# Second expert layer of a two-layer graph block: what the late row fetches wait for, when the rank products run, and where the last sums are loaded

## The chip, the cores and the metric

The kernel runs on one core of a Trainium2 chip. The metric is the device time of one execution in microseconds (us), as the median of several runs. The profile is one further execution, with the hardware profiler on. The engines are called as the profile calls them: PE (matrix products; PEld is its weight load), DVE (vector), ACT (scalar), POOL (GpSimd) and SP (the engine that does nothing here but issue transfers). A small q behind an engine's name (SPq) means its instruction sequencer, which waits, branches and issues DMAs.

## What is computed

A block of two layers over 2708 rows of 256 numbers. Each layer normalizes the rows, mixes them by an attention over a 0/1 adjacency matrix, adds the result to the rows, normalizes again, and adds the output of a mixture of eight experts, in which each row takes its two best experts. The change is in the experts of the second layer:

```python
def _L1_ffn_ref(x, gate_w, gate_b, W1, b1, W2, b2):
    logits = xf @ gate_w + gate_b
    probs = jax.nn.softmax(logits, axis=-1)
    top2_vals, top2_idx = jax.lax.top_k(probs, 2)
    cw = jnp.zeros((N, Ee), dtype=xf.dtype).at[jnp.arange(N)[:, None], top2_idx].add(top2_vals)
    def step(acc, params):
        w1, bb1, w2, bb2, we = params
        h = jax.nn.gelu(xf @ w1 + bb1, approximate=False)
        y = h @ w2 + bb2
        return (acc + we[:, None] * y, None)
...
x = x + _L1_gnn_ref(_layernorm(x, axis=-1), adj, ...)
x = x + _L1_ffn_ref((_layernorm(x, axis=-1))[None], ...)[0]
```

Here the hidden width is 512, and all numbers are float32.

## The kernel before

**Routing.** The rows form 22 tiles of 128 (the last has 20 rows). `route` (line 1437 on) is a Python generator, one per tile. It normalizes the tile, finds the two best experts of each row, and counts with two small matrix products (L1533 and L1534, the *rank products*) how many rows of earlier tiles and of this tile go to each expert. From the counts it works out a place for each row, adds the tile to the running count `seen` (L1542), and sends the rows with two indirect DMAs from POOL (L1551) to `disp`, a table in DRAM with one region per expert. Each `yield` ends a step. A `Line` holds the generators: its `step()` runs one step of each that is under way, oldest first, and starts a new one at most every `gap` steps. In the second layer most tiles are routed during the attention; the last five reach their rank products beside the experts' slots, while the flag `slots_run` is set, where `line.step()` is called twice per slot and `gap` is 2. There the power of e (L1526) is taken on POOL, and DVE sums it up in L1531.

**Slots.** The experts' work is cut into slots, each of 128 rows of one expert. The second layer has 47 that always run, numbered 0 to 46 here (`often` is 47), and up to 23 more behind a branch that these data don't take. `slot(s, s1)` issues in this order: the first product (`up`, sixteen matmuls of L1835, then four GELUs of L1843 on ACT), the transposed rows of the next slot (`turned`, L1808 on DVE), a step of the line, `down` of the slot before (eight matmuls of L1851, the scaling L1857 on DVE into one of three buffers `y`, and an indirect DMA from POOL, L1863, that writes the 128 result rows to `xd1` in DRAM), a second step of the line, and whatever is listed for this slot in `self.then`. Inside `down`, before the scaling, `fetch` issues what later slots need: rows for up to six slots ahead (`fetch_rows`: SP reads where the chunk begins, L1753, and issues four DMAs of L1760 into `xg` and one of L1766 into `who`) and the weights for three slots ahead (`fetch_weights`, L1741 on POOL, which moves nothing where the buffer already holds that expert).

**Order.** PE, ACT, DVE and SP run in the order in which the Python code issues; each engine works through its own list in order, and an instruction that waits holds up all behind it on that engine. POOL's order is the scheduler's.

**Late slots.** Slots 0 to 19 take rows of the first 14 tiles, slots 20 on take the rest. So the rows of slot 20 may be fetched only when all rows are routed. When the line is empty, `place_grid` works out on DVE which rows the slots from 20 on take, two steps per slot, and makes eight indirect DMAs on POOL (`pad_rows`, L1570) that fill up the last chunk of every expert. `self.written` collects the DMAs that must have landed: the routed rows, the pads, and also the results of L1863. In `fetch_rows`, slots 0 and 20 wait for all that `self.written` holds at that time (`behind_written`). For slot 20 these include the results of slots 0 to 12.

**Sums.** Each row's two results lie in two halves of `xd1`. For the first 16 tiles (four groups of four, `whole_`) eight loads of 512 KB are issued from SP in slot 40's `then` (L2048, `load`); they wait for the results of slots 0 to 38. In `then` of slots 43 to 46 DVE adds each group to the kept rows (`add`, L2061 and L2062) and SP stores it (`store`, L2065). The other six tiles (`rest`) form four groups. They are loaded after `experts1.run`, and so behind the branch, from SP and ACT, into the buffers of the first four groups.

**The branch.** After slot 46 every engine loads the number of used slots into a register (L1960) and jumps over the 23 conditional slots (`tc.If`, L1976). At the place it jumps to, the engines raise the semaphores by what the skipped instructions would have raised, so that the code behind sees the same counts on both ways. SP does that for the eight semaphores that its and ACT's DMAs use, and each raise waits for what was issued on that semaphore before; POOL does it for its own DMAs with one instruction of L1976 (INC_SWDGE_SEM).

Of the kernel before, what the change touches and what calls it, by code (L numbers as in the profile page):

```python
# [106 lines left out]
def adj_ffn_kernel(ctx: ExitStack, tc: tile.TileContext, a: dict, out: bass.AP):  # L107
    nc = tc.nc
# [1020 lines left out]
    class Experts:  # L1129
        def __init__(self, layer, hidden, packed_weights, gate_bias, own_norm, xd, disp, early):  # L1130
# [4 lines left out]
            nc.vector.memset(self.seen, 0.0)  # L1135
            self.routed, self.begun, self.pads = 0, False, []
            self.slots_run = False
            self.written = []
            self.groups = [f"written{layer}", f"late{layer}", f"apart{layer}", f"after{layer}", f"rows{layer}", f"summed{layer}"]
            self.early = early  # L1140
            self.side = "right" if own_norm else "left"
# [21 lines left out]
            s0 = n + size * RING  # L1163
# [258 lines left out]
                tc.declare_no_dep(start.ins, group=self.groups[2], reason="other rows of xd")  # L1422
                tc.add_to_no_dep_group(self.groups[3], start.ins)

        def behind_written(self, start, last=True, but=0):
            for ins in self.written[: len(self.written) - but]:
                tc.add_manual_dep(
                    start.ins, ins.name,
                    mybir.DependencyInfo(
                        mybir.DependencyClass.Sync, mybir.DependencyReason.DATA  # L1430
                    ),
                    reason="rows written",
                )
            if last:
                self.written = []

        def route(self, t, x, logits=None):

# [90 lines left out]
            yield  # L1529
            if self.slots_run:  # L1530
                nc.vector.tensor_reduce(den[:r, 0:1], p[:r, :k], AX.X, ALU.add)  # L1531
            ps = misc.tile([P, GROUP, P], F32, name="misc").rearrange("p g n -> p (g n)")
            nc.tensor.matmul(ps[:, :E], before, sel, start=True, stop=False)  # L1533
            nc.tensor.matmul(ps[:, :E], ones, seen, start=False, stop=True)  # L1534
# [263 lines left out]
        def slots(self, two, ps_mm, ps_acc, line):  # L1798
# [49 lines left out]
            def down(s, w, who, hT, bias2, then):  # L1848
# [12 lines left out]
                if not own_norm:  # L1861

                    start = nc.gpsimd.indirect_dma_start(  # L1863
                        xd[:], at, y, None, bounds_check=2 * N - 1, oob_is_err=False
                    )
                    for i in (2, 5):
                        tc.declare_no_dep(
                            start.ins, group=self.groups[i], reason="other rows of xd"
                        )
                    tc.add_to_no_dep_group(self.groups[2], start.ins)  # L1870
                    self.written.append(start.ins)
                    return
                start = nc.gpsimd.indirect_dma_start(  # L1873
                    xd[:], at, y, None, bounds_check=N - 1, oob_is_err=False, compute_op=ALU.add
# [98 lines left out]
            if own_norm:  # L1973
                others(often)
                return
            with tc.If(used > often):  # L1976
# [26 lines left out]
    with tc.tile_pool(name="mask", bufs=1) as mp, ExitStack() as first_masks:  # L2003
# [16 lines left out]
        with tc.tile_pool(name="sum", bufs=1, side="right") as pool:  # L2020
# [24 lines left out]
            def load(parts_, queues, early=0):  # L2045
                for i, (t, n, r) in enumerate(parts_):
                    for j, queue in enumerate(queues):
# [4 lines left out]
                            )  # L2052
                            tc.add_to_no_dep_group(experts1.groups[5], start.ins)
                        if i == 0:
                            experts1.behind_written(
                                start, last=(j == 1 and parts_ is rest), but=int(early)
                            )

            def add(t, n, r):
                y, y1 = results(t, n, r)  # L2060
# [3 lines left out]
            def store(t, n, r):  # L2064
                nc.sync.dma_start(rows_of(out, 0, t, n, r), results(t, n, r)[0])  # L2065

            def again():
                load(whole_, (nc.sync, nc.sync))
                for x in whole_:
                    add(*x)  # L2070
                    store(*x)

            experts1.again = again
            s0 = experts1.sum_behind + 2
            experts1.then = {s0: [partial(load, whole_, (nc.sync, nc.sync), 1)]}
            for i, x in enumerate(whole_):
                experts1.then[s0 + 3 + i] = [partial(add, *x), partial(store, *x)]
            experts1.run(line)
            load(rest, (nc.sync, nc.scalar))
            for x in rest:  # L2080
                add(*x)
                store(*x)
# [37 lines left out]
```

## Time and profile before

| what | value |
|---|---|
| median of three runs | 1191.05 us (1186.0 to 1194.85) |
| profiled execution, its own time | 1177.48 us |
| its span, first to last instruction | 1175.8 us |
| PE busy over the span | 1125.0 us (96%) |
| first matmul of slot 0 of the second layer's experts | at 976.9 us of the span |
| first matmul of slot 46 | at 1150.94 us |
| scaling of slot 46's results on DVE (L1857) | at 1157.45 us |
| first of the last loads on SP (L2048) | at 1165.33 us |
| last addition on DVE (L2062) | at 1172.69 us |

The table gives the span's own clock: 0 is the first instruction. The profiled execution was shorter than the median of the other three by 13.6 us, about 1%; the work and its order are the same in all of them. Between slots 28 and 43 a slot takes 3.51 us, and PE has no pause; this is the pace of the part where nothing is late.

### The profile page before, as it was taken

To read this page: it belongs to the slowest core of one execution; us is meant where nothing else is said; L and a number is where in the kernel's file an instruction comes from. 1 tells how busy PE (TensorE), PEld (TensorE's weight loads), DVE (VectorE), ACT (ScalarE), POOL (GpSimd) and SP (SyncE) were. 2 spreads that over 40 slices of the span, in tenths; PEclk is the share of its full clock that TensorE was granted. 3 is DMA by queue.
4 is the path that set the end of the run, shared out by engine and by line. 5 is a ranking of instruction groups with operands and counts; after the bars stand their busy time and mean duration, and the time that the engine had idled before them with its cause. 6 is when DMAs were issued, how large, how long until landed. Compare 5 with 4: busy or idle time off the path is not lost. (4 is left out here: it accounts for less than half of the span.)

```text
span 1175.8 us, 20858 instructions
## 1 busy us (share of the span) xinstructions
PE 1125.0 (96%) x6421; PEld 912.2 (78%) x6421; DVE 647.7 (55%) x2405; ACT 415.4 (35%) x1232; POOL 430.3 (37%) x519
## 2 busy tenths in 40 slices
PE   8989999999999999999999999998999998998993
PEld 5665666666666666789999999997899997898992
DVE  5565777786876867643222222222876777622224
ACT  3222222222222222433333333332777673344441
POOL 3001212121212122453434343423754557865552
PEclk9999999999999999999999999999999999999997
DMA  9678676867745658579675936543000517577346
GB/s 224 130 163 211 169 183 167 237 168 181 215 128 149 155 140 317 154 206 262 181 197 151 339 83 187 122 159 86 28 1 33 211 56 238 123 241 231 79 131 229
DMA packets 198661, 195.88 MB, mean 167 GB/s; under 512 B 90939, under 2 KB 181524, under 8 KB 192520
## 3 DMA queue, kind: packets, MB, share of 16 engines
q1 hardware_dynamic: 173242, 118.18, 39.7%
q0 software_dynamic: 24256, 70.81, 19.0%
q10 hardware_dynamic: 1038, 5.40, 1.3%
q8 instruction: 55, 0.90, 0.3%
q14 instruction: 70, 0.57, 0.2%
HBM read 246.19 MB, written 66.15 MB: 266 GB/s over the span
## 5 line engine op out<-in xcount | busy, mean ns | idle before, releaser
L1835 PEld LDWEIGHTS mm<-xe,ring 128*128 128x128 f32 x2192 | 260.6, 194 | 15.8 <-DVE xe L1808 5.8
L1835 PE MATMUL mm<-xe,ring 128*128 128x128 f32 x2192 | 263.9, 278 | 5.5 <-DVE xe L1808 3.9
L1843 ACT ACTIVATE hT<-mm,ring 128x128 f32<-128x128 f32 x548 | 156.6, 369 | 287.6 <-issue 157.2
L1851 PE MATMUL acc<-ring,hT 128*128 128x256 f32 x1096 | 252.1, 380 | 0.0
L1851 PEld LDWEIGHTS acc<-ring,hT 128*128 128x128 f32 x1096 | 201.6, 191 | 24.2 <-issue 0.4
L650 PEld LDWEIGHTS acc<-v,p 128*128 128x128 f32 (+1 forms) x880 | 160.0, 190 | 62.4 <-issue 37.0
L650 PE MATMUL acc<-v,p 128*128 128x257 f32 (+1 forms) x880 | 202.7, 383 | 0.0
L586 PE MATMUL s<-g,xnT 128*128 128x512 f32 x420 | 200.3, 597 | 0.6 <-DVE mT L605 0.6
L1551 POOL DMA_INDIRECT disp<-row,to x88 | 92.0, 1045 | 256.9 <-DVE x L670 125.5
L1857 DVE SCALAR_TENSOR_TENSOR y<-acc,who,bias 128x256 f32<-128x256 f32 x92 | 44.3, 481 | 254.6 <-PE acc L1851 232.9
L288 POOL TENSOR_TENSOR ln_rs<-ln_rs,minus_half 128x2 f32<-128x2 f32 x88 | 68.7, 782 | 172.9 <-DVE ln_rs L284 120.4
L598 ACT ACTIVATE p<-s 128x512 f32<-128x512 f32 x105 | 62.7, 597 | 194.8 <-PE s L586 178.7
L930 PE MATMUL acc<-parts,m 128*128 128x266 f32 x924 | 126.2, 293 | 0.0
L930 PEld LDWEIGHTS acc<-parts,m 128*128 128x128 f32 x924 | 117.1, 185 | 4.1 <-ACT raw L957 0.9
L586 PEld LDWEIGHTS s<-g,xnT 128*128 128x128 f32 x420 | 76.8, 190 | 55.1 <-issue 50.3
L1741 POOL DMA_INDIRECT ring<-L_ffn_packed,weight_row x76 | 80.2, 1055 | 92.4 <-PE acc L1851 61.8
L601 DVE SCALAR_TENSOR_TENSOR p<-p,mT 128x512 f32<-128x512 f32 x100 | 71.0, 710 | 75.3 <-ACT p L598 75.2
L1873 POOL DMA_INDIRECT xd<-y,who x45 | 71.2, 1583 | 111.3 <-DVE xe L1814 50.2
L897 ACT CAST m<-mT 128x512 fp32r<-128x512 fp8e4 (+4 forms) x168 | 71.8, 475 | 9.7 <-PE acc L930 6.3
L1863 POOL DMA_INDIRECT xd<-y,who x47 | 50.3, 1071 | 48.6 <-DVE y L1857 44.8
L272 DVE SCALAR_TENSOR_TENSOR row<-x,wr_rows 128x256 f32<-128x256 f32 x128 | 54.4, 425 | 3.3
L1814 DVE TENSOR_SCALAR xe<-xe_raw,ring 128x128 f32<-128x128 f32 x90 | 27.7, 352 | 40.2 <-DMA ring<-L_ffn_packed,weight_row 39.2
(337 smaller groups left out, 1073.1 us busy)
## 6 DMA issues: line engine op xcount, KB each, us to landing
adj<-in_adj_dram SPq DMA_DIRECT2D x100, 256.0 KB
L_ffn_packed<-in_L_ffn_W_dram SPq DMA_DIRECT2D x32, 512.0 KB
xg<-disp SPq DMA_DIRECT2D x368, 32.0 KB
L_ffn_packed<-in_L_ffn_W_dram SPq DMA_DIRECT2D x32, 256.0 KB
neighbours<-mT SPq DMA_DIRECT2D x5, 1408.0 KB
mT<-neighbours SPq DMA_DIRECT2D x5, 1408.0 KB
ring<-L_ffn_packed SPq DMA_DIRECT2D x3, 2182.0 KB
xin<-in_x_dram SPq DMA_DIRECT2D x42, 128.0 KB
```

The source lines that it names most:

```text
L288: nc.gpsimd.tensor_tensor(rs[:r, 1], rs[:r, 0], minus_half[:r], ALU.pow)
L586: nc.tensor.matmul(ps[:kr, :nb], xnT[:, c, k0 : k0 + kr], g[:, c, :nb], start=(c == 0), stop=(c == DC - 1 and k < KEYS),)
L601: nc.vector.scalar_tensor_tensor(p, p, LARGEST, mask, op0=ALU.min, op1=ALU.mult)
L650: nc.tensor.matmul(accs[j][:r], p[keys, q0 : q0 + r], v[keys, k, :], start=(k == 0), stop=(k == NT - 1),)
L897: nc.scalar.copy(m[:, : q1 - q0], MASKS[b].of_key(mTs[b], k)[:, q0 - b * BN : q1 - b * BN],)
L930: nc.tensor.matmul(acc[:r], masks[t], parts[:, k, i], start=(k == 0 and i == 0), stop=False,)
L1551: nc.gpsimd.indirect_dma_start(disp[:], bass.IndirectOffsetOnAxis(ap=to[:r, j : j + 1], axis=0), rows2[:r, j], None,)
L1741: nc.gpsimd.indirect_dma_start(w, None, packed[:], bass.IndirectOffsetOnAxis(ap=self.weight_row[:, s : s + 1], axis=0), bounds_check=E * P ...
L1835: nc.tensor.matmul(ps[:, i, :], w[:, c * hidden + f * P : c * hidden + (f + 1) * P], xe[:, c, :], start=(c == 0), stop=(c == DC - 1),)
L1843: nc.scalar.activation(hT[:, f, :], ps[:, i, :], AF.Gelu, bias=w[:, b1 + f : b1 + f + 1])
L1851: nc.tensor.matmul(ps, hT[:, f, :], w[:, w2 + f * D : w2 + (f + 1) * D], start=(f == 0), stop=(f == hc - 1),)
L1873: start = nc.gpsimd.indirect_dma_start(xd[:], at, y, None, bounds_check=N - 1, oob_is_err=False, compute_op=ALU.add)
```

## The change

Five things are done to the second layer's experts:

- `self.results` is a list of its own for the DMAs that write results. `self.written` keeps the routed rows and pads. So slot 20's row fetch waits for rows and pads alone, and the loads of the sums wait for results alone.
- In `route`, for the tiles of the second layer that are routed beside the slots, one more `yield` stands ahead of the rank products. They, and all that follows in the tile (the places, `seen`, the two DMAs of L1551), come one step of the line later.
- The loads of the last four groups (`load(rest, ...)`) are issued ahead of `tc.If`, behind the loading of the register, as `self.ending()`.
- In the branch's body, which these data skip, the last four groups are loaded again, from SP.
- The additions and stores of the first four groups are listed for slots 42 to 45 in place of 43 to 46. Their loads stay with slot 40.

```diff
-            self.written = []
+            self.written, self.results = [], []
...
-        def behind_written(self, start, last=True, but=0):
-            for ins in self.written[: len(self.written) - but]:
+        def behind_results(self, start, but=0):
+            self.behind(start, self.results[: len(self.results) - but])
+
+        def behind_written(self, start, last=True):
+            self.behind(start, self.written)
+            if last:
+                self.written = []
+
+        def behind(self, start, written):
+            for ins in written:
                 tc.add_manual_dep(
...
             if self.slots_run:
                 nc.vector.tensor_reduce(den[:r, 0:1], p[:r, :k], AX.X, ALU.add)
+            if self.slots_run and not own_norm:
+                yield
             ps = misc.tile([P, GROUP, P], F32, name="misc").rearrange("p g n -> p (g n)")
             nc.tensor.matmul(ps[:, :E], before, sel, start=True, stop=False)
             nc.tensor.matmul(ps[:, :E], ones, seen, start=False, stop=True)
...
-                    self.written.append(start.ins)
+                    self.results.append(start.ins)
...
+            self.ending()
             with tc.If(used > often):
...
                         if i == 0:
-                            experts1.behind_written(
-                                start, last=(j == 1 and parts_ is rest), but=int(early)
-                            )
+                            experts1.behind_results(start, but=int(early))
...
                 for x in whole_:
                     add(*x)
                     store(*x)
+                load(rest, (nc.sync, nc.sync))
 
             experts1.again = again
+            experts1.ending = partial(load, rest, (nc.sync, nc.scalar))
             s0 = experts1.sum_behind + 2
             experts1.then = {s0: [partial(load, whole_, (nc.sync, nc.sync), 1)]}
             for i, x in enumerate(whole_):
-                experts1.then[s0 + 3 + i] = [partial(add, *x), partial(store, *x)]
+                experts1.then[s0 + 2 + i] = [partial(add, *x), partial(store, *x)]
             experts1.run(line)
-            load(rest, (nc.sync, nc.scalar))
             for x in rest:
                 add(*x)
                 store(*x)
```

`self.sum_behind` is 38, so `s0` is 40.

More of the change, by code (lines that the diff above doesn't have):

```diff
@@ L1433, in behind_written @@
                 )
-            if last:
-                self.written = []
         def route(self, t, x, logits=None):
```

## The prediction

> **What bounds the kernel now.** I read the page first, then the busy time by windows of the second layer's experts, then the chain of waits there, then the waits of single engines, last the timeline of the end. The page names PE:
>
> ```profile
> PE 1125.0 (96%) x6421; PEld 912.2 (78%) x6421; DVE 647.7 (55%) x2405; ACT 415.4 (35%) x1232; POOL 430.3 (37%) x519
> ```
>
> So nothing is to be won but where PE pauses. The change touches only what lies behind 976.9 us; the windows there (PE, PEld, DVE, ACT, POOL busy, PE clock, DMA share, GB/s) show where PE is not full:
>
> ```profile
> 1036.00:1052.00 16.00, 16.00 (x110) 14.99 (x109) 3.34 (x8) 7.44 (x25) 11.23 (x11) 1.00 0.99 359
> 1052.00:1064.00 12.00, 12.00 (x86) 11.36 (x85) 3.52 (x8) 4.87 (x16) 6.43 (x7) 1.00 0.43 94
> 1064.00:1080.00 16.00, 14.20 (x96) 12.64 (x94) 3.03 (x7) 6.49 (x20) 8.25 (x9) 1.00 1.02 341
> 1140.00:1157.00 17.00, 16.35 (x107) 14.67 (x105) 12.37 (x16) 6.16 (x21) 7.71 (x5) 1.00 0.96 354
> 1157.00:1162.00 5.00, 0.00 (x0) 0.00 (x0) 0.93 (x2) 0.00 (x0) 1.12 (x2) 0.64 0.43 140
> 1162.00:1165.00 3.00, 0.00 (x0) 0.00 (x0) 0.00 (x0) 0.00 (x0) 0.00 (x0) 0.50 0.03 8
> ```
>
> Two bursts of weights fill the DMA engines (1036 to 1052 and 1064 to 1080); PE pauses in the second only. Behind 1157 there are 8 us with almost no work at all. The chain says what the pause in the second burst hangs on; SP's and DVE's waits give the size:
>
> ```profile
> 1038.96 7.67 DMA xd<-y,who
> 1046.82 6.82 DMA xg<-disp
> ...
> 1062.22 6.05 DMA xg<-disp
> ...
> 1069.63 7.78 DMA xg<-disp
> 1077.43 5.96 DMA xg<-disp
> ```
> ```profile
> SPq L1760 <- DMA xd<-y,who: 5.8, 1, 5.8
> ```
> ```profile
> DVE xe L1808 <- DMA xg<-disp: 15.2, 7, 4.5
> ```
>
> Slot 12's result landed 7.67 us after its issue, SP stood 5.8 us for it, and every later row fetch was late by that. The timeline has the price: slots 24 to 28 begin at 1069.75, 1073.65, 1079.00, 1084.01 and 1087.6, where 3.51 us is the pace, so 0.39 + 1.84 + 1.50 + 0.1 = 3.8 us are lost.
>
> The end, by the timeline of DVE and of the two loading queues, and by the instructions of L1976:
>
> ```profile
> 1140.53 0.48 DVE L1857 SCALAR_TENSOR_TENSOR y<-acc,who,bias 128x256 f32<-128x256 f32 x1 [2.68 <-PE acc L1851]
> 1140.93 0.43 DVE L1808 STREAM_TRANSPOSE xe<-xg 128x256 f32<-128x256 f32 x1
> 1144.04 0.48 DVE L1857 SCALAR_TENSOR_TENSOR y<-acc,who,bias 128x256 f32<-128x256 f32 x1 [2.68 <-PE acc L1851]
> 1144.44 1.22 DVE L2061 TENSOR_TENSOR y<-y,kept 128x1024 f32<-128x1024 f32 x1
> 1157.45 0.48 DVE L1857 SCALAR_TENSOR_TENSOR y<-acc,who,bias 128x256 f32<-128x256 f32 x1
> ```
> ```profile
> 1165.33 1.73 SPq L2048 DMA_DIRECT2D y<-xd  x4
> 1165.40 1.98 ACTq L2048 DMA_DIRECT2D mT<-xd  x4
> 1168.77 0.69 DVE L2061 TENSOR_TENSOR y<-y,kept 128x512 f32<-128x512 f32 x1 [10.84 <-DMA mT<-xd]
> ```
> ```profile
> L1976 SPq EVENT_SEMAPHORE  x9: 17/17/17, 1162.1 to 1162.6; - x9
> L1976 PEldq COMPARE_BRANCH  x1: 4557/4557/4557, 1156.3 to 1156.3; - x1
> L1976 SPq COMPARE_BRANCH  x1: 50/50/50, 1158.3 to 1158.3; - x1
> L1976 POOLq INC_SWDGE_SEM  x1: 1617/1617/1617, 1163.4 to 1163.4; - x1
> ```
>
> Slot 46's result lands at 1161.96 by the trace's completion events, but the loads start only when POOL's INC_SWDGE_SEM is done (1163.4 + 1.6 = 1165.0). SP is back from its branch 3.75 us after it (1158.3 to 1162.1).
>
> **The change part by part.** I write times on the clock of before and carry a shift.
>
> *Row fetch of slot 20.* Its wait was the whole 5.8 us: SP was ready at 1040.5, routed rows and pads had landed by 1028.6. SP then runs 5.8 us ahead. In a burst a fetch takes SP some 4.6 us instead of 2.97 (L1753 starts of fetches 25 to 29: 1064.22 to 1082.61), because each of the eight DMA semaphores must be free again; so 5.8 us are 1.3 fetches, and in the quiet part 1.3 x 3.18 us (mean pace of fetches 29 to 46) = 4.1 us. Of the 3.8 us lost I give back 3.5: rows of slot 28, issued near 1072 and landing some 8 us later, become the latest, about 0.3 us late. Ends: 3.8, all of it, and 1.3, if the rows of slot 28 land when those of 27 do now (1083.4, 2.5 us too late). The weights are not next: those of slot 29, the last of the burst, land at 1082.9, needed at 1087. PE: -3.5.
>
> [...]
>
> *Rank products.* For five tiles two matmuls (0.17 us each), seven short DVE operations (some 1.2 us) and two POOL DMAs (1.03 us each) come half a slot later; nothing is added. PE's waits for them between 976 and 1010 are:
>
> ```profile
> PE misc L1533 <- DVE sel L1523: 3.2, 3, 1.6
> PE misc L1534 <- DVE seen L1542: 1.5, 2, 0.7
> ```
>
> Most is covered: PE would have waited for the transposed rows anyway (1.6 us at 987.9: rows ready 988.27, products done 988.1). Visible are 0.5 us each at 994.3 and 1004.5. But DVE still waits for POOL's power in L1531 (7.3 us in 4 waits), and POOL works without a gap there. The last tile ends behind the check of slot 6, so placing starts in slot 7, one slot (3.5 us) later: rows of slots 20 on are placed at 1026.5, SP reads them at 1040.5; the weight rows at 1028.5, POOL reads them at 1028.3, cover gone, 0.2 us off the path. I take -0.3. Ends: -1.0 (both visible waits), and +2 if POOL puts results behind the pads; a result that waits like this already cost DVE 3.95 us and PE 0.8 us at slot 13.
>
> *Early sums a slot sooner.* Same eight additions (1.22 us each), four stores. The first would start behind slot 41's scaling, at 1140.93 - 3.5 - 0.3 = 1137.1. Its rows: loads start behind SP's last fetch, 1139.71 - 4.1 = 1135.6; the first landed 3.8 us after its issue (1139.71 to 1143.50, by the completion events), so 1139.4. DVE waits 2.3 us, and the transposed rows of slot 44 are queued behind it. These now start at 1140.93 with 2.4 us to spare before slot 44's matmuls at 1143.84, and the additions use 2.45 up. So the wait is PE's: +2.3. The second load of the group lands 1.3 us after the first, in time; later groups come every 2.6 us against 3.5 us per slot. Ends: 0, if SP gets all 5.8 us, to +6.4, if it keeps none of its lead. On the other side the last addition no longer stands before slot 46's scaling: PE ends at 1156.35, the scaling began at 1157.45, -1.0. Sum at that scaling: -3.5 - 0.3 + 2.3 - 1.0 = -2.5, so 1154.95. The stores leave SP a slot sooner and are landed when the loads reuse their buffers.
>
> *Last loads ahead of the branch.* They wait for slot 46's result only: 0.75 us to its issue, then 2.4 us (as 1134.27 to 1136.68; it took 3.75 beside the last store): 1158.1. Four DMAs each on SP and ACT, 0.3 us to the first and 1.75 on SP; behind them SP has its branch, then the raising of the semaphores, then the stores; ACT nothing that matters. The additions are written after a second load inside the skipped branch, so I read them as waiting for SP's raising: 1158.1 + 2.1 + 3.75 + 0.6 = 1164.6. The last load lands 6.7 us after the release (1165.0 to 1171.69): 1164.8. I take 1165.0 for the first addition, against 1168.77: -3.8, of which -2.5 came in. Ends: 1161.9, if landing alone releases (3.77 us as now), and 1166.4, if the way back takes 5.5 us like ACT's (branch 1154.4, next record 1159.9, in full DMA traffic). From there the additions run on (4.3 us), as now.
>
> [...]
>
> **Sum.** -3.8 us on the profiled execution: 1177.48 to 1173.7, its span 1175.8 to 1172.0. That execution stands 13.6 us below the median of the runs, with the same stages; I carry the difference over: 1191.05 - 3.8 = 1187.2.
>
> **The rivals.**
>
> *Landing alone frees the last additions* (0.2). Then 1161.9 + 4.3 in place of 1165.0 + 4.3: 3.1 us more, 1184.1. For it: L2061 now ends its idle time by a DMA; against: the second load in the branch.
>
> *The early addition blocks DVE* (0.15), the slower side. Without its wait the parts give 3.5 + 0.3 + 1.0 + 1.3 = 6.1 us; each us of the loads beyond 1133.3 takes one back. Slower than before once they start later than 1139.4, that is, if SP keeps under 0.3 us of its lead. At 1141 it costs 7.7: 1192.7. For it: SP is at its limit in both bursts; against: 5.8 us is a long lead to lose.
>
> *The row wait stays* (0.1): slot 20 still waits for something of POOL. No lead, no 3.5; the addition starts at 1140.6 at the soonest, its rows land at 1143.5, DVE waits 2.9, and 1.0 + 1.3 + 0.3 come back: +0.3, 1191.3.
>
> The forecast has the remaining 0.55, alone 1184.7 to 1189.7 (its ends, mostly offsetting: later PE means less wait).
>
> **Range.** All gains together (3.8 + 1.0 + 1.0 + 4.4) make -10; the blocked DVE (+1.6) and the worst of the rank products (2.3 off the forecast) make +4; the three runs scatter by -5 and +4 around their median. 1180.0 to 1194.0 holds the cases and most of that scatter. About 1% is what a measurement can tell from no change. No case reaches 11.9 us alone; with scatter I give 0.06 to faster, 0.05 to slower, 0.89 within.
>
> **What would show it.** Right: SP's wait on xd at L1760 gone; slots 24 to 28 at 3.5 us; a DVE wait for a load before slot 42's addition; L2048 on SP ahead of its branch, near 1158; the first of the last additions 6 to 8 us after that. Wrong: rows still awaited at slots 25 to 27; no DVE wait at slot 42; the last additions 3 to 4 us behind their loads; new pauses between slots 8 and 16.

## The result, and the profile after

| | kernel before | changed kernel |
|---|---|---|
| median, 7 runs each | 1190.78 us (1186.0 to 1194.85) | 1186.9 us (1185.35 to 1191.36) |
| ratio to before, run beside run | | 0.9994, 95% interval 0.9972 to 1.0016 |
| both again, 35 and 12 runs, another occasion | 1179.74 us | 1180.58 us, ratio 1.0017, interval 1.0000 to 1.0035 |

The first runs can't tell the two apart; the second interval reaches from no difference to a loss of 4 us. The two occasions are 11 us apart for the same kernel. The traces say why, and one needs that to read everything below. The profiled execution of the changed kernel took 1186.24 us (span 1184.4):

```profile
span 1184.4 us, 20859 instructions
...
PE 1128.4 (95%) x6421; PEld 915.8 (77%) x6421; DVE 645.8 (55%) x2405; ACT 413.4 (35%) x1232; POOL 428.5 (36%) x519
```

Busy time hardly moved, the span is 8.6 us longer than that of before. By windows (PE, PEld, DVE, ACT, POOL busy, PE clock, DMA share, GB/s), first before, then the changed kernel, then a second execution of the *unchanged* kernel (e1 below):

```profile
1010.00:1022.00 12.00, 11.71 (x82) 10.96 (x81) 9.15 (x37) 4.93 (x17) 8.95 (x11) 1.00 0.49 119
1022.00:1036.00 14.00, 13.34 (x92) 12.22 (x91) 6.32 (x27) 5.84 (x20) 10.95 (x11) 1.00 0.52 125
```
```profile
1010.00:1022.00 12.00, 9.57 (x61) 8.95 (x60) 5.15 (x23) 3.07 (x10) 7.70 (x9) 0.88 0.40 103
1022.00:1036.00 14.00, 9.96 (x55) 9.01 (x55) 4.99 (x17) 3.07 (x10) 9.29 (x10) 0.87 0.41 104
```
```profile
1010.00:1022.00 12.00, 9.87 (x54) 8.66 (x53) 3.21 (x15) 2.56 (x9) 9.25 (x10) 0.86 0.40 96
1022.00:1036.00 14.00, 6.78 (x25) 5.16 (x24) 5.86 (x22) 2.97 (x10) 7.21 (x7) 0.66 0.39 103
```

In the last two all engines do less at once, at a DMA share of 0.4. These are pauses that cost 10 to 15 us in slots 7 to 12. (Here and below, what a stretch of slots *loses* is its length, from first matmul to first matmul, less 3.51 us per slot.) The changed kernel's first trace and e1 to e4 have them, with the change and without it; e5 to e12 have not (0.6 to 2.0 us lost there), again with it and without it. So they belong to the occasion, not to the change, and totals are compared only within an occasion. The trace that the prediction read has no such pauses either (1.5 us), although the runs listed with it took 1186 to 1195 us; the record does not say why.

What the change did shows in the waits and timelines. SP's waits from 1000 to 1060: the 5.8 us for xd are gone (the unchanged kernel has them in e1 as well), and this is the only line left:

```profile
SPq L1768 <- DMA xg<-disp: 2.1, 2, 2.0
```

DVE's timeline at the first early addition (L2068), which now stands behind slot 41's scaling, and the end, with the instructions of the branch (L1985):

```profile
1147.19 0.48 DVE L1865 SCALAR_TENSOR_TENSOR y<-acc,who,bias 128x256 f32<-128x256 f32 x1 [2.68 <-PE acc L1859]
1149.76 1.23 DVE L2068 TENSOR_TENSOR y<-y,kept 128x1024 f32<-128x1024 f32 x1 [2.08 <-DMA y<-xd]
1151.11 1.23 DVE L2069 TENSOR_TENSOR y<-y,mT 128x1024 f32<-128x1024 f32 x1
1152.25 0.44 DVE L1816 STREAM_TRANSPOSE xe<-xg 128x256 f32<-128x256 f32 x1
```
```profile
1165.39 0.48 DVE L1865 SCALAR_TENSOR_TENSOR y<-acc,who,bias 128x256 f32<-128x256 f32 x1 [1.24 <-PE acc L1859]
1166.15 0.97 POOL L1871 DMA_INDIRECT xd<-y,who  x1 [0.75 <-DVE y L1865]
1169.85 3.58 SPq L2057 DMA_DIRECT2D y<-xd  x4
...
1177.88 1.29 DVE L2068 TENSOR_TENSOR y<-y,kept 128x512 f32<-128x512 f32 x2 [12.01 <-SPq L1985]
```
```profile
L1985 SPq EVENT_SEMAPHORE  x9: 17/17/17, 1177.0 to 1178.0; - x9
...
L1985 SPq COMPARE_BRANCH  x1: 50/50/50, 1173.5 to 1173.5; - x1
```

DVE waits 2.08 us for the load, and the transposed rows of slot 44 stand behind it. At the end SP issues the loads, goes to its branch at 1173.5, is back at 1177.0, and the first of the last additions follows SP's raising, 12.5 us behind the last scaling; before it was 11.3.

For all traces the same stages are read from the timeline. *Lost* is the time by which the first matmuls of these slots come later than at the pace of 3.51 us. The upper block has the pauses, the lower has not.

```
                        lost in slots            slot 46    scaling to    scaling    span
kernel             0-6   7-12  23-27  41-45   to scaling  first of last   to end
e1 before again    6.9   14.9   0.0    0.1       6.5          11.4        18.6     1188.2
e2 rows alone      6.9   14.5   3.1    0.5       6.5          11.4        18.7     1192.8
changed            8.0   10.6   0.0    2.5       5.5          12.5        19.1     1184.4
e3 sums back       8.3   12.3   0.0    1.3       6.5          12.7        19.2     1185.3
e4 no second load  8.0   10.8   0.0    7.2       5.5          11.7        18.3     1188.0

before             6.9    1.5   3.8    0.1       6.5          11.3        18.3     1175.8
e5 rank back       6.9    0.9   0.6    8.0       5.5          11.9        18.5     1180.2
e6 loads behind    7.9    0.6   4.7    3.8       5.5          11.3        18.3     1181.2
e7 best ahead      8.0    0.6   1.2    0.2       5.4           9.7        19.6     1173.1
e8 best behind     8.0    0.6   1.6    0.1       5.4          12.2        18.9     1175.1
e9 changed again   8.0    0.6   2.6    4.0       5.5          12.1        18.7     1179.4
e10 rows alone     6.9    2.0   2.4    0.1       6.5          12.1        19.1     1177.4
e11 fourth alone   6.9    0.9   3.4    0.1       5.4          12.3        19.2     1174.0
e12 rows, fourth   7.0    1.5   0.0    3.9       5.4          12.0        19.2     1181.1
```

The spans also differ by where slot 0 begins (976.1 to 982.4), which lies ahead of the change. One trace each: a figure that differs by a few tenths between them says nothing.

### The profile page after: what moved, and what is told of

It is laid out like the page before. It is cut to its first block, busy times and chain, and to the rows that moved or that the text cites. A ratio compares the mean times of both kernels' runs of the same rounds, so it can differ in the third digit from the quotient of the medians.

```text
span 1184.4 us, 20859 instructions
## 1 busy us (share of the span) xinstructions
PE 1128.4 (95%) x6421; PEld 915.8 (77%) x6421; DVE 645.8 (55%) x2405; ACT 413.4 (35%) x1232; POOL 428.5 (36%) x519
## 3 DMA queue, kind: packets, MB, share of 16 engines
q0 software_dynamic: 24256, 70.81, 18.9%
## 5 line engine op out<-in xcount | busy, mean ns | idle before, releaser
L1843 PEld LDWEIGHTS mm<-xe,ring 128*128 128x128 f32 x2192 | 263.1, 195 | 20.1 <-DVE xe L1816 11.0
L1843 PE MATMUL mm<-xe,ring 128*128 128x128 f32 x2192 | 265.9, 279 | 11.1 <-DVE xe L1816 8.6
L1749 POOL DMA_INDIRECT ring<-L_ffn_packed,weight_row x76 | 80.0, 1052 | 94.7 <-PE acc L1859 63.9
L1871 POOL DMA_INDIRECT xd<-y,who x47 | 49.5, 1052 | 55.4 <-DVE y L1865 52.6
```

The costliest lines, as they stand in the source:

```text
L1749: nc.gpsimd.indirect_dma_start(w, None, packed[:], bass.IndirectOffsetOnAxis(ap=self.weight_row[:, s : s + 1], axis=0), bounds_check=E * P ...
L1843: nc.tensor.matmul(ps[:, i, :], w[:, c * hidden + f * P : c * hidden + (f + 1) * P], xe[:, c, :], start=(c == 0), stop=(c == DC - 1),)
```

## The experiments

Theory: the change trades 1 to 4 us at the late rows for as much at the early additions; the last loads win nothing; the pauses are not its own. The rivals stand with each run. The runs e1 to e4, e5 to e8 and e9 to e12 were made on three occasions; the median of the kernel before was 1188.59, 1179.73 and 1179.74 us on them. Each occasion was another chip (numbers 10, 9 and 12), so what belongs to an occasion may belong to its chip.

**e1, the kernel before once more.** No edit.

> The kernel before, unchanged, run and profiled once more. It is to say which differences between the two traces belong to the change. My theory: the pauses of 10.5 us that the trace of the changed kernel shows in slots 7 to 12 belong to that execution, not to the change, so another execution of the kernel before may show some of them (lost in slots 7 to 12: anything from 1 to 12 us); what belongs to the kernel is the 3.8 us lost in slots 23 to 27, the 0.1 us lost in slots 41 to 45, 6.5 us from slot 46's first matmul to its scaling, and 11.3 us from there to the first of the last additions; these come again within 0.5 us. The rival: the pauses belong to the change, so here slots 7 to 12 lose 1.5 us again, and the time is near 1177. Ratio to the kernel before: 1 within 0.3% by both.

Ratio 1.0012 (0.9987 to 1.0037). 14.9 us are lost in slots 7 to 12: the pauses are not the change's. But one part of my theory fell: slots 23 to 27 lose 0.0 us here, not 3.8. While PE pauses, SP's lead over PE (first matmul of a slot less the start of its fetch) grows to 20.6 us at slot 20, from 15.2 us in the trace of before, and the wait on xd is paid out of it. So in this trace, with the pauses, the row part had nothing to win.

**e2 and e10, the row part alone**, on two occasions. The edit to the kernel before, beside the two helpers `behind_results` and `behind` of the change:

```diff
-                    self.written.append(start.ins)
+                    self.results.append(start.ins)
...
-                            experts1.behind_written(
-                                start, last=(j == 1 and parts_ is rest), but=int(early)
-                            )
+                            experts1.behind_results(start, but=int(early))
```

> The kernel before with the one part that slot 20's row fetch waits for routed rows and pads alone. My theory: the loss of 3.8 us in slots 23 to 27 becomes 0 to 0.5 us, the rest stays as before (11.3 us from the last scaling to the first of the last additions), so 3.5 us less than the kernel before. The rival (the weights' bursts leave the earlier fetches no room): 1.5 to 2.5 us stay lost in slots 23 to 27, so 1.3 to 2.3 us less. A second rival (the row fetch's new place brings the pauses in slots 7 to 12): these lose 10 us here too.

> The kernel before with the row part alone, once more, for a trace without the pauses. My theory: the wait of 5.8 us that is gone stood beside the first weights' burst; SP now stands in that burst one fetch later, its four row DMAs taking some 8 us, and leaves it with a lead of 0.5 to 3 us more. Slots 23 to 27 lose 0.6 to 4.7 us in place of 3.8, so 0 to 3 us less than before. The rival (the prediction): the lead lasts, slots 23 to 27 lose 0.3, and 3.5 us are won.

Ratios 1.0014 (0.9995 to 1.0033) and 0.9999 (0.9981 to 1.0016): no gain clear of the noise either time. Slots 23 to 27 lose 3.1 and 2.4 us, where the kernel before lost 0.0 with pauses and 3.8 without them. In e2 my theory fell (3.1 us lost, not 0 to 0.5), and the first rival's figures did too: more stayed lost than its 1.5 to 2.5 us, and its gain of 1.3 us or more is outside the interval. SP's lead at slot 20 was only 13.5 us in that trace, 20.6 in e1, so the two say little of the edit. The second rival falls: slots 7 to 12 lose 14.5 us in e2 and 14.9 without the edit in e1. The theory of e10 holds for the loss (0.6 to 4.7 us); slot 21's row DMAs took 5.6 us there, not 8. Where the lead went is shown below, under the row fetch.

**e3, the early additions back at slots 43 to 46.**

```diff
-                experts1.then[s0 + 2 + i] = [partial(add, *x), partial(store, *x)]
+                experts1.then[s0 + 3 + i] = [partial(add, *x), partial(store, *x)]
```

> The changed kernel with the additions and stores of the first four groups back at slots 43 to 46. My theory: the 2.45 us lost in slots 41 to 45 go, because DVE no longer stands before a load that has not landed, and the last addition stands before slot 46's scaling again (6.5 us from its first matmul in place of 5.5), so 1.4 us less than the changed kernel. The rival: the loads come late by so much that DVE waits at slot 43 as well, and 1 to 2 us stay lost; then no gain, up to 1 us more. What lies behind the scaling is as in the changed kernel (12.5 us to the first of the last additions).

Ratio 0.9987 (0.9966 to 1.0008). Slots 41 to 45 lose 1.3 us, inside the rival's 1 to 2: the loads began 8.2 us behind slot 41's first matmul, where it was 6.3 in the changed kernel's trace, and DVE waited 0.69 and 0.35 us at slot 43 as well. The size is open by one trace.

**e4, no second load in the branch.** It leaves out a load that only the branch would need; these data don't take it.

```diff
-                load(rest, (nc.sync, nc.sync))
```

> The changed kernel without the second load of the last four groups inside the branch. It leaves out what would be needed if the branch were taken; these data don't take it, so the work done is the same. My theory: the last additions wait for SP's raising of the semaphores only because of that second load. Without it they begin when their rows have landed, 2 to 3 us after the first load's issue, so some 8 us behind the last scaling in place of 12.5, and the kernel ends 3.5 to 4.5 us sooner than the changed one. The rival: every reader behind the branch stands behind the raising, whatever the branch holds; then the 12.5 us stay, SP's return of 3.5 us and the raising of 1.1 us among them, and nothing is gained.

Ratio 1.0001 (0.9979 to 1.0023). The rival's figures hold: SP's raising and, by the timeline, the first addition, 11.7 us behind the last scaling:

```profile
L1985 SPq EVENT_SEMAPHORE  x9: 17/17/17, 1181.3 to 1181.8; - x9
...
L1985 SPq COMPARE_BRANCH  x1: 50/50/50, 1177.3 to 1177.3; - x1
```
```profile
1181.47 1.29 DVE L2068 TENSOR_TENSOR y<-y,kept 128x512 f32<-128x512 f32 x2 [11.23 <-SPq L1985]
```

The addition comes 0.2 us behind the beginning of the raising, with no second load there. So the second load is not the reason for the wait. That it comes whatever the branch holds is not shown: the skipped code of e4 still loads the first four groups, into the same buffers, and a branch that leaves these buffers alone was not run.

**e5, the rank products back in their old step.**

```diff
-            if self.slots_run and not own_norm:
-                yield
```

> The changed kernel with the rank products in their old step (the added yield taken out); all else as changed. In the six traces so far the loss in slots 0 to 6 is 6.92 to 6.94 us without the yield and 7.95 to 8.27 us with it, and in slots 7 to 12 it is 14.5 and 14.9 us without it and 10.6 to 12.3 us with it (1.5 us in the first trace of before, which has no such pauses). My theory: both belong to the yield. Then this kernel loses 6.9 us in slots 0 to 6 and about 14.5 in slots 7 to 12, and is 2 to 3 us slower than the changed one. The rival: the pauses of slots 7 to 12 differ by execution and only the 1.0 us of slots 0 to 6 belongs to the yield; then slots 7 to 12 lose some 11 us as in the changed kernel, and this one is 1 us faster.

Ratio 1.0011 (0.9988 to 1.0034). My theory fell for the second half: there are no pauses on this occasion with or without the yield, 0.9 us in slots 7 to 12. The 1.0 us of slots 0 to 6 is the yield's: 6.9 us in seven traces without it, 7.9 to 8.3 in seven with it. Slots 41 to 45 lost 8.0 us here, the most of all, so the time says nothing of the yield.

**e6, the last loads behind the branch again.**

```diff
-            self.ending()
...
-                load(rest, (nc.sync, nc.sync))
...
             experts1.run(line)
+            load(rest, (nc.sync, nc.scalar))
```

> The changed kernel with the last loads behind the branch again, and without the second load in it. In three traces with the loads behind the branch the first of the last additions came 11.3 to 11.4 us behind the last scaling, in three with them ahead 11.7 to 12.7. My theory: ahead of the branch, SP can go to its branch only when it has waited for the last result and issued the loads, so that its way back of 3.5 to 4.8 us follows the result's landing in place of running beside it; here it runs beside it again, so 11.3 us, 1.2 less than the changed kernel's trace. The rival: what differs is how long the result took to land in those executions (3.6 to 4.0 us); then the first addition comes 12 us or more behind the scaling here too.

Ratio 1.0012 (0.9993 to 1.0030). The timeline of the end:

```profile
1162.93 0.48 DVE L1865 SCALAR_TENSOR_TENSOR y<-acc,who,bias 128x256 f32<-128x256 f32 x1 [1.24 <-PE acc L1859]
...
1170.55 1.73 SPq L2056 DMA_DIRECT2D y<-xd  x4
1170.62 1.98 ACTq L2056 DMA_DIRECT2D mT<-xd  x4
1174.20 0.69 DVE L2067 TENSOR_TENSOR y<-y,kept 128x512 f32<-128x512 f32 x1 [10.79 <-DMA mT<-xd]
```

The 11.3 us are back, as the theory says. Over all traces: 11.3, 11.4, 11.4, 11.3 and 12.1 us with the loads behind the branch and the fourth addition ahead of slot 46's scaling (before, e1, e2, e6, e10), and 12.5, 12.7, 11.7, 11.9, 12.1 with them ahead (changed, e3, e4, e5, e9). The two ranges overlap by e10, whose last result landed 4.4 us behind its issue, against 3.75 in before; to that extent the rival holds. Of the 0.7 us in the mean, most comes back: with the loads ahead all rows have landed when the additions start, so that these and the stores take 6.56 us to the end in place of 7.0 to 7.2.

**e7 and e8, two versions made from this.** Both have additions at slots 43 to 45 and the fourth behind slot 46's scaling, where DVE has nothing to do. e7 also does the last additions and stores ahead of the branch; e8 has the last loads behind it. Of e7's edit:

```diff
...
-            experts1.ending = partial(load, rest, (nc.sync, nc.scalar))
+            def ending():
+                add(*whole_[3])
+                store(*whole_[3])
+                load(rest, (nc.sync, nc.scalar))
+                for x in rest:
+                    add(*x)
+                    store(*x)
+            experts1.ending = ending
...
-            for i, x in enumerate(whole_):
-                experts1.then[s0 + 2 + i] = [partial(add, *x), partial(store, *x)]
+            for i, x in enumerate(whole_[:3]):
+                experts1.then[s0 + 3 + i] = [partial(add, *x), partial(store, *x)]
             experts1.run(line)
-            for x in rest:
-                add(*x)
-                store(*x)
```

> A version made from what was seen: the changed kernel, with three additions at slots 43 to 45, the fourth behind slot 46's scaling, where DVE has nothing to do, and the last additions and stores ahead of the branch as well (in the branch, which these data don't take, they are done once more). My theory: the last additions then wait for their rows alone. Slot 46 takes 5.5 us to its scaling; the loads are issued 4.0 to 4.5 us behind it and landed 2.5 us later, so the first of the last additions comes 7 to 8 us behind the scaling in place of 12.5; the stores end 4 to 5 us later, and then SP still has its branch, 3.5 to 4.8 us, and the raising: the span ends 16 to 18 us behind the scaling, where the changed kernel took 19.05. With 1 us less in slots 41 to 45, some 2 to 3 us less in all. The rival: the branch at the end costs as much as it did between; 19 us, and only the 1 us is won.

> The other version: the changed kernel with the last loads behind the branch, three additions at slots 43 to 45 and the fourth behind slot 46's scaling, ahead of the branch. My theory: slots 41 to 45 lose 0 to 1.3 us in place of 2.45 or more, slot 46 takes 5.5 us to its scaling, and the first of the last additions comes 11.3 us behind that; the span ends 18.3 us behind the scaling; 1.5 to 3.5 us less than the changed kernel. The rival: SP's branch now waits for the fourth addition (2.5 us behind the scaling), so its return is later by 1.5 us and ends last; then 12 to 13 us to the first addition, and 0 to 1.5 us are won.

Ratios 0.9990 (0.9971 to 1.0010) and 0.9991 (0.9972 to 1.0010). In e7's timeline the addition waits for its rows at last:

```profile
1158.77 5.44 SPq L2057 DMA_DIRECT2D y<-xd  x4
...
1163.15 0.69 DVE L2068 TENSOR_TENSOR y<-y,kept 128x512 f32<-128x512 f32 x1 [5.64 <-DMA y<-xd]
```

That is 9.7 us behind the scaling (my theory had 7 to 8; the loads went out 5.3 us behind it); with e4 it shows that the branch, not the transfer, held the additions. But the branch then stands at the end: the span ends 19.6 us behind the scaling, where the changed kernel took 18.7 and 19.1. The rival was right about the end. In e8 the first of the last additions came 12.2 us behind the scaling and the end 18.9, where my theory had 11.3 and 18.3: the rival's figures, but its cause is not shown, as the loads went out only 0.2 us later than in before. What both traces win on the changed kernel is in slots 41 to 45 (0.2 and 0.1 us lost) and in slot 46 (5.4 us).

**e9, the changed kernel once more.** No edit.

> The changed kernel, unchanged, run and profiled once more, for its trace in an execution without the pauses of slots 7 to 12. My theory, from the traces without them: slots 0 to 6 lose 8.0 us, slots 7 to 12 0.6, slots 23 to 27 0.6 to 4.7 (before: 3.8), slots 41 to 45 2.5 to 8 (before: 0.1), slot 46 takes 5.5 us to its scaling (before: 6.5), and the span ends 18.3 to 19.2 us behind that (before: 18.3): within 4 us of the kernel before on either side, 1.000 to 1.003 of its time. The rival (the prediction): slots 23 to 27 lose 0.3, slots 41 to 45 2.3, and 3.8 us are won.

Ratio 1.0017 (1.0000 to 1.0035), as the theory says; the 3.8 us of the prediction (0.9968) are outside of it. Against the trace of before, stage by stage: slot 0 begins 1.6 us later, +1.0 in slots 0 to 6, -0.9 in 7 to 12, -0.1 in 13 to 22, -1.2 in 23 to 27, +3.9 in 41 to 45, -1.0 in slot 46, +0.3 to the end: +3.6, which is the difference of the spans.

**e11 and e12, the fourth addition alone, and with the row part.** The edits to the kernel before (e12 has those of e10 as well):

```diff
             in_a_row(0, often)
+            for start in self.then.get(often, ()):
+                start()
...
-            for i, x in enumerate(whole_):
+            for i, x in enumerate(whole_[:3]):
                 experts1.then[s0 + 3 + i] = [partial(add, *x), partial(store, *x)]
+            experts1.then[experts1.often] = [partial(add, *whole_[3])]
             experts1.run(line)
+            store(*whole_[3])
             load(rest, (nc.sync, nc.scalar))
```

> The kernel before with one new edit: the fourth of the early additions stands behind slot 46's scaling, where DVE has nothing to do, and its store behind the branch; the first three stay at slots 43 to 45. My theory: slot 46 takes 5.5 us to its scaling in place of 6.5, and DVE's way back from the branch, 2.5 us later, is still hidden behind the last loads, so the span ends 18.3 to 18.9 us behind the scaling: 0.5 to 1 us less than before. The rival: the store ahead of the last loads on SP holds these up, and the end gives the 1 us back.

> The row part and the fourth addition's new place together, with the rank products, the early loads and the last loads as in the kernel before: what is left when the parts that cost are taken out. My theory: 0 to 3 us from the rows and 0.5 to 1 us from the addition, so 0.5 to 4 us less than before, and slots 41 to 45 lose 0.1 us. The rival: as the lead is spent in the bursts, the rows give nothing, and only 0.5 to 1 us is won.

Ratios 0.9995 (0.9975 to 1.0014) and 0.9988 (0.9973 to 1.0003). Slot 46 reaches its scaling 1.1 us sooner in both, and the end takes 0.9 us more: the rival of e11. SP's four last loads take 5.3 and 5.5 us to issue behind that store, 1.7 in before; but e10, with no such store, has an end of 19.1 us too, so the size is open. No version here is faster than the kernel before beyond its interval. e12's trace shows the trade in one kernel: no loss at all in slots 23 to 27, and 3.9 us in slots 41 to 45 (my theory: 0.1) although its additions stand a slot later. PE is early there, SP is not, and DVE waits 2.0 us for the load.

## Why the prediction was right, and where it was not

The forecast was a difference within 1%, at 1187.2 us, and that came. The reasons carry it only in part. The late rows, the early sums and slot 46's scaling have the sign that was forecast, the rank products and the last loads have not; and the early sums take back more than the rows win, where the rows were to win. That the median fell on 1187 is luck and no proof of the 3.8 us: run beside run the ratio is 0.9994, not 0.9968. Of the signs named ahead, e9 shows the right ones for the wait on xd, for DVE's wait and for the last loads (the first addition 7.9 us behind their issue), and one of the wrong ones: rows are still awaited, as PE stops 1.64 us ahead of slot 26 and 0.43 ahead of slot 27.

**Row fetch.** The wait went, as said. Mis-sized was the lead that it leaves, taken as 4.1 us in the quiet part. SP's timeline before, then in e9 (xg are the rows, four DMAs per slot):

```profile
1046.82 1.86 SPq L1760 DMA_DIRECT2D xg<-disp  x4
1048.95 0.36 SPq L1766 DMA_DIRECT2D who<-disp  x1
1049.86 4.11 SPq L1760 DMA_DIRECT2D xg<-disp  x4
1054.23 0.35 SPq L1766 DMA_DIRECT2D who<-disp  x1
1055.08 1.85 SPq L1760 DMA_DIRECT2D xg<-disp  x4
```
```profile
1041.64 3.30 SPq L1768 DMA_DIRECT2D xg<-disp  x4
1045.20 0.36 SPq L1774 DMA_DIRECT2D who<-disp  x1
1046.43 8.54 SPq L1768 DMA_DIRECT2D xg<-disp  x4
1055.43 0.35 SPq L1774 DMA_DIRECT2D who<-disp  x1
1056.28 1.86 SPq L1768 DMA_DIRECT2D xg<-disp  x4
```

and SP's waits of e9 from 1030 to 1070:

```profile
SPq L1768 <- DMA xg<-disp: 6.5, 4, 2.8
...
SPq L1768 <- DMA who<-disp: 2.0, 1, 2.0
```

Before, SP stood 5.8 us for xd and then issued slot 20's rows at 1046.82 and slot 21's at 1049.86. In e9 slot 20's go out at 1041.64, 5.2 us sooner (though slot 0 begins 1.6 us later there), and slot 21's take 8.54 us, from 1046.43 to 1055, 6.8 of them in three waits for earlier fetches of its own (xg and who above). In the traces of before and of the changed kernel SP's DMAs raise eight semaphores (101 to 108) in turn, and a DMA waits for the one that raised its semaphore before: in before, slot 20's first row DMA goes out at 1046.82, raises its semaphore for the last time at 1053.63, and the next DMA on it, slot 21's fourth, goes out at 1053.65. The DMA share from 1036 to 1052 is 0.94 in e9, 0.99 before. Slot 22's rows go out at 1055.08 before and at 1056.28 in e9: the lead is spent one fetch later. In numbers of the two traces, SP's lead over PE is 9.9 and 15.2 us at slot 21, 8.1 and 8.5 at slot 22, 9.6 and 9.3 at slot 31. So SP's stall of 5.8 us in that stretch was not a cost of its own; it stood beside the burst. Slots 23 to 27 lose 0.0 to 4.7 us (the latter in e6, with 1.7 of it at half clock) in the seven traces with the row part and no pauses (mean 1.9), and 3.8 and 3.4 without it (before, e11): some 1.8 us won, not 3.5, by traces that scatter widely. At slot 22 the lead is 7.9 to 11.3 us in those seven and 8.1 and 8.6 in the two. The times can't show a gain of this size (e10's interval reaches down to 2.2 us less). Of the prediction's figures the lower end, 1.3 us, was nearer: e9 won 1.2.

**Rank products.** Forecast -0.3; measured +1.0 in slots 0 to 6 and -0.9 in 7 to 12 of e9, together +0.1, inside the ends. (Slots 7 to 12 lose 0.9 to 2.0 us in the five traces with the old step and no pauses, 0.6 in the four with the new one.) PE's waits from 976 to 1012, in e9 and then in e10, which has the old step:

```profile
PE mm L1843 <- DVE xe L1816: 3.8, 2, 2.7
PE mm L1843 <- DVE den L1544: 1.1, 1, 1.1
PE misc L1542 <- DVE seen L1550: 0.7, 1, 0.7
```
```profile
PE misc L1539 <- DVE sel L1529: 2.5, 2, 1.7
PE misc L1540 <- DVE seen L1548: 2.0, 3, 0.7
PE mm L1841 <- DVE xe L1814: 0.2, 1, 0.2
```

Most of the waits for the products are gone, and PE waits for transposed rows instead. The timeline of e9, then of e10:

```profile
1001.89 1.68 POOL L1532 TENSOR_TENSOR p<-euler,p 128x8 f32<-128x8 f32 x1
...
1003.60 0.16 DVE L1537 TENSOR_REDUCE den<-p 128x1 f32<-128x8 f32 x1 [2.96 <-POOL p L1532]
...
1005.15 0.45 DVE L1816 STREAM_TRANSPOSE xe<-xg 128x256 f32<-128x256 f32 x1
...
1005.65 2.90 PE L1843 MATMUL mm<-xe,ring 128*128 128x128 f32 x16 [2.66 <-DVE xe L1816]
```
```profile
1004.01 0.16 DVE L1537 TENSOR_REDUCE den<-p 128x1 f32<-128x8 f32 x1 [2.06 <-POOL p L1532]
...
1005.49 0.45 DVE L1814 STREAM_TRANSPOSE xe<-xg 128x256 f32<-128x256 f32 x1
1005.51 0.17 PE L1539 MATMUL misc<-sel,before 128*128 128x8 bf16 x1 [0.77 <-DVE sel L1529]
...
1006.43 0.17 PE L1540 MATMUL misc<-seen,ones 128*128 128x8 bf16 x1 [0.75 <-DVE seen L1548]
```

In both, DVE's wait for POOL's power (L1532) stands ahead of a slot's transposed rows. In e10 PE is held by the products there, 0.8 us or less at a time, and the rows are ready when it comes to them; in e9 it comes sooner and idles 2.66 us. The prediction named DVE's wait, and did not ask what would come to stand behind it. It also took a wait of PE at its length alone. Behind this one the sixteen matmuls of L1843 take 2.90 us, where 1.95 is usual, and the next eight 2.76 where 1.89 is: the granted clock is 0.5 for 3.41 us from 1006.65 on. Half of these 3.41 us is 1.7, most of the 1.9 that slot 6 loses. All seven traces with the yield have this pause (2.65 or 2.66 us) and a stretch at half clock behind it.

**Early sums a slot sooner.** The mechanism is the one predicted, and in e9 so is the size of the wait. SP's loads were taken 4.1 us sooner; counted from slot 0's first matmul they began at 162.8 us before, and at 161.4 in e9, 1.4 sooner. But PE is only 1.2 us sooner at slot 41 in place of 3.8, so the loads begin 6.3 us behind slot 41's first matmul, where the forecast comes to 6.1 (1135.6 less 1129.5), and slot 43 loses 2.27 us for the forecast 2.3. What the prediction put at nothing is what follows the pause of PE. In the changed kernel's first trace, and then in e9, with e9's window (columns as above) last:

```profile
1152.74 2.05 PE L1843 MATMUL mm<-xe,ring 128*128 128x128 f32 x16 [2.07 <-DVE xe L1816]
```
```profile
1146.48 3.68 PE L1843 MATMUL mm<-xe,ring 128*128 128x128 f32 x16 [2.11 <-DVE xe L1816]
```
```profile
1146.48:1150.16 3.68, 3.68 (x17) 3.68 (x18) 3.02 (x4) 0.00 (x0) 1.70 (x1) 0.54 1.03 412
```

The same sixteen matmuls take 3.68 us at a granted clock of 0.54, and slot 44 loses 1.73 us more in e9; in the changed kernel's first trace the clock stayed at 1.00 and slot 44 lost 0.1. So 4.0 us are lost in slots 41 to 45 in place of 2.3, and 2.5 to 8.0 (mean 5.1) in the five traces with this edit (changed, e4, e5, e6, e9). Both parts vary: slot 43 loses 2.0 to 2.3 us where the loads begin 5.9 to 6.3 us behind slot 41's first matmul (e6, e9, changed), and 5.5 and 5.7 where they begin 9.3 behind it (e4, e5); slot 44 loses 1.5 to 2.3 us more in four of the five. The ends were 0 and +6.4, the latter if SP "keeps none of its lead"; two traces are beyond it. This is the rival "the early addition blocks DVE", at its place, with less than its price in e9. The last addition off slot 46's scaling gave the 1.0 us, 6.5 to 5.5.

**Last loads ahead of the branch.** Forecast 10.05 us from the scaling to the first addition, measured 12.5 and, in e9, 12.1: 4.2 to the loads' issue (0.75, then a landing of 3.5 where 2.4 was taken), 3.6 for SP's issue (1.75 and 0.3 taken: one load alone took 2.2 us to issue), 3.2 for the way back (3.75 taken), 1.1 of raising (0.6 taken). That SP's way back decides was right, against the rival in which landing alone frees the additions; that the second load is the reason was wrong (e4). The prediction's upper end was a way back of 5.5 us, as long as ACT's "in full DMA traffic". With the loads ahead it took 3.2 to 4.8 us in five traces, and 3.3 to 5.2 in the eight with them behind, so these runs show no such lengthening. And the step missed the comparison: before, that way back ran *beside* the landing of the last result (1158.3 to 1162.1, landed at 1161.96); behind the loads it runs after it (e9: loads from 1164.97, branch at 1168.6, back at 1171.8). So +0.8 us, not -1.3; the quicker additions leave +0.3.

**The sum.** By the terms of e9: -1.2 + 0.1 + 3.9 - 1.0 + 0.3, and -0.1 between, make +2.0 us, where -3.8 was forecast. Of these 5.8 us, the rows' lead that was not kept makes 2.3, the early sums 1.6 (the half clock behind their pause), the last loads 1.6 and the rank products 0.4. The size of each is that of one pair of traces.

**The execution that was read.** The step "with the same stages; I carry the difference over" was the other weak one. The 13.6 us between the profiled execution and the median fit the pauses of slots 7 to 12 (13.4 us more in e1 than in the trace of before), though the executions behind that median left no trace; and the pauses change what the parts are worth: in e1 slot 20's wait costs PE nothing. No new pauses came from the change, though the prediction's list would have read those of the first trace as one.

## What to carry to other kernels

The wait of 5.8 us that ended inside a burst of transfers (DMA share 0.99) was worth some 1.8 us here, 1.2 in e9: follow the queue to the far end of the congested stretch and compare the lead there before counting such a wait. The loads that were moved ahead of the branch held up the branch of SP, which issues them: it came 8.1 us behind the last scaling in the changed kernel's first trace, 0.8 before; ask what the way back was hidden behind. Where a change makes PE pause, read the granted clock and the length of the matmuls behind the pause too: here that part cost 1.7 us behind a pause of 2.1. And when the profiled execution stands 1% off the median, profile the unchanged kernel twice before explaining a change with one trace.

## What the runs showed of the hardware

- Half clock behind a pause. Stretches of 3.41 us at a granted clock of 0.5 followed pauses of PE: in the changed kernel's first trace behind 2.65, 2.43 and 2.75 us (from 1005.50, 1019.16 and 1032.81 on), in e9 behind 2.66 and 2.11, in e6 behind 2.68 and 1.88, in e12 behind 2.00. Sixteen matmuls, 1.95 us elsewhere, took 3.68 in the second of e9, at a mean clock of 0.54. Not every pause brought one: none followed 2.07 us in the changed kernel's first trace (clock 1.00 from 1152 to 1160), 2.88 at slot 27 in e2, or 1.64 at slot 26 in e9. What decides it was not tried.
- Pauses that belong to an occasion. In e1 PE is busy 6.78 us of the 14 from 1022 to 1036, in before 13.34. The five traces with pauses also lack records of raised semaphores: 1025 to 1027 for PE's, where the nine others have 1149 to 1156. Engines go on together (in the changed kernel ACT at 1032.05, POOL at 1032.07 and DVE at 1031.83). What holds them is not shown by any view, and no run was made for it; whether the chip, the time or the recording itself has a part stays open.
- The last indirect DMA of results took 3.4 to 4.0 us from its issue to the loads that wait for it with next to nothing else under way (changed kernel 3.70, e4 4.03, e5 3.35, e9 3.45), and 4.5 in e3 and e7, which have one more store of SP's beside it; the prediction had taken 2.4 from a like one.
- The way round the skipped branch took SP 2.8 (e7) to 5.2 us (e11); 3.8 in before, 3.5 in the changed kernel's first trace. The first of the last additions, which reads what loads ahead of the branch have brought, waited 11.23 us to SP's raising where it stands behind the branch (e4), and 5.64 to its own load where it stands ahead (e7), here with a branch whose skipped code writes the same buffers.
